# Entmax of the second batch: its power issued a step earlier in the mixture of experts

## The chip, the cores and the metric

The kernel runs on one NeuronCore of a Trainium2 chip. Five instruction streams work side by side: TensorE (PE in the profile, its weight loads as PEld), VectorE (DVE), ScalarE (ACT), GpSimd (POOL) and SyncE (SP), which issues most of the DMAs. They wait for each other through semaphores. The metric is the device time of one execution in microseconds; the time before is the median of three runs, 2685.04 us (2682.86 to 2685.15).

## The reference

The kernel is a two-layer decoder on `x` of 2 batches x 1024 tokens x 256, all in float32, each sublayer followed by a layer norm of the sum with its input: attention, cross attention with an MLP, a mixture of experts, attention again, cross attention again, and a feed-forward with fake quantisation. What matters here is the mixture of experts:

```python
logits = (xt @ Wr + br) / TEMP              # 2048 tokens x 8 experts
gates = entmax_bisect(logits)               # alpha = 1.5: p = max(x/2 - tau, 0)^2, sums to 1
gates = jnp.where(gates > THRESH, gates, 0.0)
h = jax.nn.relu(jnp.einsum('td,edf->etf', xt, W1) + b1[:, None, :])
y = jnp.einsum('etf,efd->etd', h, W2) + b2[:, None, :]
out = jnp.einsum('etd,te->td', y, gates)
```

Every expert is computed for every token and weighted by its gate. For alpha = 1.5 the threshold tau has a closed form over the sorted logits, with one square root per candidate; the kernel uses that in place of the bisection.

## The kernel before

The tokens are worked on in four groups `g` of 512; groups 0 and 1 are the first batch, 2 and 3 the second. The experts' stage (`l0_ffn`, line 806) runs 33 rounds `n` over `steps = (expert, group)`, expert outermost. Round n computes the hidden layer of step n and at the same time the second product of step n - 1. "First step" is n = 0, "second step" n = 1, "third step" n = 2, as one counts from one.

Both products use a Strassen-like scheme: seven products of half-sized blocks in place of eight, with sums of blocks as operands. The hidden layer's products are written (z, k) here: half z, block product k (matmuls at line 885, results in PSUM tiles `unit`). The second product's are written as plain k (matmuls at line 933, results in the PSUM tiles `acc` for k = 1, 6, 7, 4 and `bank` for k = 2, 5, 3). One tile takes its products one after the other, each added onto the last; VectorE reads it between two of them (line 942, scaled by the gate), and the next product on that tile can begin only when that read is over. The order of the 21 products in a round is a list, with positions i from 0:

```python
order = (
    (0, 1), (0, 2), (1, 1), (1, 2), 1, (0, 6), 2, (0, 5), (1, 6), 6, (1, 5), (0, 7), 5, (1, 7),
    7, (0, 3), (0, 4), 4, (1, 3), (1, 4), 3,
)
```

What each position issues beside its matmuls: ScalarE copies units to SBUF for k = 1, 6, 7 (lines 892, 896, 898) and applies the relu (874); VectorE adds units for k = 2, 7, 3 (lines 894, 899, 902), finishes k = 4 (908) and reads the second product (942). At the end of a round `sums` (line 914) forms the operand sums of the step just made: lines 783 and 784 on VectorE, then 785 and 786 on GpSimd. Line 783's result is needed by product 5 of the next round, 785's by product 6, 786's by product 3, 784's by product 7.

A dictionary `jobs` maps positions to other work, called right after the product at that position. The entmax is a generator, `self.entmax(b)` (line 712), cut into pieces by `yield`. For the second batch (`gates`, line 954) the pieces are called here: 1 and 2, four `max` each (line 743); 3, four small VectorE instructions (lines 746 to 749); 4, seven more (751 to 758) and then the square root, a power with exponent 0.5 of 128 x 64 elements on GpSimd (759); 5, four VectorE instructions of which the first reads the power's result (761 to 764); 6, seven more that finish the gates (766 to 772). The gates of the second batch are first read at the start of round n = 3 (`begin`, line 836).

TensorE, VectorE and ScalarE take their instructions in the order in which this code issues them (`manual_schedule`, line 967). GpSimd's and SyncE's queues are ordered by the framework's planner, by priority and by when it expects their inputs. An engine works through its queue in order: an instruction that waits holds all that is behind it.

Of the kernel before, what the change touches and what calls it, by code (L numbers as in the profile page):

```python
# [32 lines left out]
class Decoder:  # L33
# [772 lines left out]
    def l0_ffn(self):  # L806
        nc, t = self.nc, self.t
        HT = GT // 2
        with ExitStack() as s:
# [6 lines left out]
            def load(e):  # L816
                w1[e] = self.weight(t["L0_ffn_W1"][e].rearrange("(c p) f -> p c f", p=P), 2, 4 * D)
                w2[e] = self.weight(t["L0_ffn_W2"][e].rearrange("(f p) d -> p f d", p=P), 8, D)

            def first(e):  # L820
                w, h = w1.pop(e), 2 * D
                sums = self.gp.tile([P, 3, h], F32, tag="w1s", name="w1s")
                up[e] = self.left(
                    (nc.gpsimd, nc.gpsimd), w[:, 0, 0:h], w[:, 1, 0:h], w[:, 0, h : 2 * h],
                    w[:, 1, h : 2 * h], [sums[:, k, :] for k in range(3)],
                )

            def second(e):
                w, h = w2.pop(e), D // 2
                sums = self.gp.tile([P, 3, 4, h], F32, tag="w2s", name="w2s")  # L830
                down[e] = self.right(
                    nc.gpsimd, w[:, 0:4, 0:h], w[:, 0:4, h:D], w[:, 4:8, 0:h], w[:, 4:8, h:D],
                    [sums[:, k] for k in range(3)],
                )

            def begin(b):
                gT = one.tile([E, S], F32, tag="gT", name="gT")
                for h in range(2):
                    ps = self.bank()
                    for i in range(4):  # L840
                        nc.tensor.transpose(
                            ps[0:E, i * P : (i + 1) * P], self.gates[b][:, 4 * h + i, :], self.ident
                        )
                    self.evac(gT[:, h * GT : (h + 1) * GT], ps[0:E, :])
                    yield
                for h in range(2):
                    g = 2 * b + h
                    a = accs[g] = self.rp.tile([P, 4, D], F32, tag="r", name="r")
                    for i in range(0, 4, 2):
                        ps = self.bank().rearrange("p (i d) -> p i d", i=2)  # L850
                        for k in range(2):
                            n = h * 4 + i + k
                            nc.tensor.matmul(
                                ps[:, k, :], lhsT=gT[:, n * P : (n + 1) * P], rhs=self.mb2,
                                start=True, stop=True,
                            )
                        nc.vector.tensor_tensor(
                            a[:, i : i + 2, :], ps, self.x[g][:, i : i + 2, :], ALU.add
                        )
                    yield  # L860
# [53 lines left out]
            def sums(e, g):  # L914
                h = act.pop((e, g))
                s = one.tile([P, 3, 4, HT], F32, tag="hs", name="hs")
                engines = (nc.vector, nc.vector if (e, g) == steps[-1] else nc.gpsimd)
                return self.left(
                    engines, h[:, 0:4, 0:HT], h[:, 4:8, 0:HT], h[:, 0:4, HT:GT],
                    h[:, 4:8, HT:GT], [s[:, k] for k in range(3)],  # L920
                )

            def gather(e, g, h):

                ps = [None, None]

                def product(k):
                    at = int(k in (2, 5, 3))
                    if k in (1, 2):
                        ps[at] = self.bank() if at else self.acc()  # L930
                    for m in range(2):
                        for c in range(4):
                            nc.tensor.matmul(  # L933
                                ps[at][:, m * P : (m + 1) * P], lhsT=h[k][:, c, m * P : (m + 1) * P],
                                rhs=down[e][k][:, c, :], start=k in (1, 2, 5) and m + c == 0,
                                stop=True, skip_group_check=True,
                            )
                    i, d = {1: (0, 0), 2: (0, 0), 6: (0, 1), 3: (0, 1), 4: (1, 0), 5: (1, 1), 7: (1, 1)}[k]
                    for m in range(2):
                        a = accs[g][:, 2 * i + m, d * P : (d + 1) * P]  # L940
                        gate = self.gates[g // 2][:, g % 2 * 4 + 2 * i + m, e : e + 1]
                        nc.vector.scalar_tensor_tensor(  # L942
                            a, ps[at][:, m * P : (m + 1) * P], gate, a, ALU.mult, ALU.add
                        )

                return product
# [7 lines left out]
            gates = self.entmax(1)  # L954
# [5 lines left out]
            def normed(g):  # L960
                self.x[g] = self.layernorm(accs[g])

            def turned(g):
                nxT[g] = self.transposed(self.x[g])

            engines = {mybir.EngineType.PE, mybir.EngineType.DVE, mybir.EngineType.Activation}
            with self.tc.manual_schedule(engines=engines):
                start = [begin(b) for b in range(B)]
                mixed = None
                for n in range(len(steps) + 1):  # L970
                    jobs = {}
                    for k in range(4):
                        if n in (0, 3):
                            jobs[k] = lambda: next(start[n // 3])
                    if n == 0:
                        jobs[5], jobs[9] = self.last_group
                    if n in (1, 2):
                        for k in range(3):
                            jobs[4 + 4 * k] = lambda: next(gates)
                    if n > 3:  # L980
                        jobs[14] = lambda: next(ready, None)
                    if n >= len(steps) - NG + 2:
                        g = n - (len(steps) - NG + 2)
                        if n < len(steps):
                            jobs[5], jobs[17] = (lambda: normed(g)), (lambda: turned(g))
                    a = hidden(*steps[n]) if n < len(steps) else None
                    b = gather(*steps[n - 1], mixed) if n else None
                    if n % NG == 1 and n // NG + 1 < E:
                        load(n // NG + 1)
                    for i, k in enumerate(order):  # L990
                        if isinstance(k, int):
                            if b:
                                b(k)
                        elif a:
                            a(*k)
                        if i in jobs:
                            jobs[i]()
                    if n == 0:
                        for _ in start[0]:
                            pass  # L1000
                        self.tokens(2)
                        self.tokens(3)
                    if n == 2:
                        for _ in gates:
                            pass
                    if n % NG == NG - 1 and n // NG + 1 < E:
                        first(n // NG + 1)
                    if n % NG == 0 and 0 < n < len(steps):
                        second(n // NG)
                    if a:  # L1010
                        mixed = sums(*steps[n])
                for _ in ready:
                    pass
                for g in range(2, NG):
                    normed(g)
# [738 lines left out]
```

## Time and profile before

| | us |
|---|---|
| median of three runs | 2685.04 |
| the profiled execution's own time | 2682.37 |
| its span, first to last instruction | 2680.6 |
| TensorE busy | 2562.0 (96%) |
| VectorE busy | 1641.2 (61%) |
| ScalarE busy | 1151.9 (43%) |
| GpSimd busy | 798.1 (30%) |
| mean granted TensorE clock | 0.97 |
| one power of the entmax on GpSimd, line 759 | 10.55 |
| `sums` on VectorE, line 783, median of 32 | 1.218 |
| `sums` on GpSimd, line 786, median of 31 | 2.350 |

The profile is of one execution. Times in it count from the start of the span. A timeline row gives start, length, engine, line of the kernel, operation, output and inputs with their shapes, and how many instructions are merged; in brackets stands how long the engine had been idle before, and what ended that. The granted clock is the share of full speed that TensorE was given. TensorE's lengths are modelled from pipelined matmuls, so neighbouring rows overlap a little.

### The profile page before, as it was taken

The numbers are of one execution on the slowest core, as the hardware profiler recorded it, in microseconds if no ns is written. First come the engines' busy times: TensorE is split into PE (matmuls) and PEld (weight loads), VectorE is DVE, ScalarE is ACT, GpSimd is POOL, SyncE is SP. The second block draws the span as 40 slices with busy tenths as digits, with TensorE's granted clock in tenths as the row PEclk, the third lists the DMA queues.
The fourth block names the chain that finished last, engine by engine and source line by source line (L and its number), as shares of the span: only waits on it lengthen the run. The fifth ranks groups of instructions, "written<-read, shape, count | busy, mean of one in ns | idle before, by whom it ended". The sixth has DMA issues, their size and how long they took to land. (4 is left out here: it accounts for less than half of the span.)

```text
span 2680.6 us, 41386 instructions
## 1 busy us (share of the span) xinstructions
PE 2562.0 (96%) x16113; PEld 1910.0 (71%) x16113; DVE 1641.2 (61%) x3204; ACT 1151.9 (43%) x1808; POOL 798.1 (30%) x615
## 2 busy tenths in 40 slices
PE   8999999999999999899999999999979999998975
PEld 5777777777777656688999999999954444444652
DVE  4666566666656532245555565554667978895686
ACT  4555455545545522122333333333315655664344
POOL 3344344334444321242333333342311000100421
PEclk9999999999999999998999999999988999999996
DMA  4223223222322020100010010010030321110000
GB/s 123 60 56 83 54 54 70 60 54 64 76 54 50 15 75 16 34 5 17 24 32 17 27 33 32 12 44 5 1 61 3 59 37 32 32 33 1 1 1 32
DMA packets 87906, 102.95 MB, mean 38 GB/s; under 512 B 39496, under 2 KB 57504, under 8 KB 87712
## 3 DMA queue, kind: packets, MB, share of 16 engines
q1 hardware_dynamic: 87200, 99.27, 16.2%
q8 instruction: 128, 2.10, 0.3%
q10 hardware_dynamic: 512, 1.05, 0.2%
q14 instruction: 66, 0.54, 0.1%
HBM read 34.21 MB, written 2.10 MB: 14 GB/s over the span
## 5 line engine op out<-in xcount | busy, mean ns | idle before, releaser
L339 POOL TENSOR_SCALAR p<-p,rs 128x1024 f32<-128x1024 f32 x256 | 287.1, 1122 | 524.2 <-DVE rs L338 524.1
L1126 DVE TENSOR_REDUCE most<-bank 128x1 f32<-128x512 f32 x512 | 325.9, 685 | 55.2 <-PE bank L1120 47.1
L325 DVE TENSOR_REDUCE nm<-wide 128x1 f32<-128x1024 f32 x256 | 311.8, 1219 | 65.2 <-PE wide L311 44.6
L330 ACT ACTIVATE p<-wide,nm 128x1024 f32<-128x1024 f32 x256 | 286.1, 1118 | 96.3 <-DVE rs L338 85.2
L1169 ACT ACTIVATE w<-wide 128x1024 f32<-128x1024 f32 x256 | 248.3, 1022 | 138.1 <-PE wide L1163 129.4
L74 ACT COPY w<-bank 128x512 f32<-128x512 f32 x260 | 152.2, 586 | 321.6 <-PE bank L352 317.2
L352 PEld LDWEIGHTS bank<-ident,p 128*128 128x128 f32 x2048 | 232.6, 141 | 66.8 <-POOL p L339 25.0
L352 PE MATMUL bank<-ident,p 128*128 128x128 f32 x2048 | 270.8, 275 | 3.7 <-ACT w L74 2.2
L311 PE MATMUL wide<-k,q 128*128 128x512 f32 x960 | 252.4, 404 | 3.4 <-ACT p L330 3.4
L70 DVE COPY w<-bank 128x512 f32<-128x512 f32 x260 | 179.1, 689 | 107.7 <-PE bank L352 98.9
L373 PE MATMUL acc<-w,v 128*64 128x256 f32 x2048 | 237.8, 384 | 0.1
L874 ACT ACTIVATE mhT<-mhT,cols 128x256 f32<-128x256 f32 (+1 forms) x256 | 143.2, 607 | 149.9 <-DVE mhT L902 98.9
L373 PEld LDWEIGHTS acc<-w,v 128*64 128x64 f32 x2048 | 143.1, 137 | 76.5 <-issue 12.7
L311 PEld LDWEIGHTS wide<-k,q 128*128 128x128 f32 x960 | 171.2, 189 | 36.5 <-ACT p L330 5.4
L885 PE MATMUL unit<-xT,w 128*128 128x256 f32 x768 | 183.5, 381 | 0.0
L785 POOL TENSOR_TENSOR hs<-hs,mhT 128x1024 f32<-128x1024 f32 x31 | 103.4, 3336 | 262.0 <-DVE hs L783 262.0
L942 DVE SCALAR_TENSOR_TENSOR r<-acc,gates,r 128x128 f32<-128x128 f32 x256 | 77.8, 346 | 140.5 <-PE acc L933 140.5
L1120 PE MATMUL bank<-kst,qst 64*128 64x512 f32 x512 | 149.6, 483 | 12.4 <-DVE most L1126 12.1
L1120 PEld LDWEIGHTS bank<-kst,qst 64*128 64x128 f32 x512 | 70.3, 193 | 121.4 <-DVE most L1126 95.2
L885 PEld LDWEIGHTS unit<-xT,w 128*128 128x128 f32 x768 | 141.3, 191 | 17.2 <-issue 0.7
L181 POOL TENSOR_TENSOR rstd<-ve,nhalf 128x4 f32<-128x4 f32 (+2 forms) x28 | 26.1, 932 | 391.6 <-DVE ve L179 391.2
L1183 PE MATMUL acc<-w,v 128*32 128x512 f32 x1024 | 137.0, 607 | 0.0
(321 smaller groups left out, 4412.1 us busy)
## 6 DMA issues: line engine op xcount, KB each, us to landing
k<-xg SPq DMA_DIRECT2D x240, 128.0 KB, 2.4
w<-in_L_ffn_W SPq DMA_DIRECT2D x16, 1024.0 KB, 5.3
q<-xg SPq DMA_DIRECT2D x120, 128.0 KB, 2.3
qst<-qh SPq DMA_DIRECT2D x60, 64.0 KB, 2.4
qst<-ql SPq DMA_DIRECT2D x60, 64.0 KB, 2.4
kst<-kh SPq DMA_DIRECT2D x60, 64.0 KB, 2.9
kst<-kl SPq DMA_DIRECT2D x60, 64.0 KB, 2.4
xg<-in_x SPq DMA_DIRECT2D x4, 512.0 KB, 4.4
```

The costliest lines, as they stand in the source:

```text
L70: nc.vector.tensor_copy(out, in_)
L74: nc.scalar.copy(out, in_)
L311: nc.tensor.matmul(sc[h][:, kb, :], lhsT=qs[u, h, qt // 4][:, at : at + P], rhs=ks[u, h][i][:, kb * 512 : (kb + 1) * 512], start=i == 0, s ...
L325: nc.vector.tensor_reduce(nm, sc, AX.XY, ALU.max, negate=True)
L330: nc.scalar.activation(p, sc.rearrange("p a c -> p (a c)"), AF.Exp, bias=nm, accum_out=sum_)
L339: nc.gpsimd.tensor_scalar(p, p, rs, 1.0, ALU.mult, ALU.mult)
L352: nc.tensor.transpose(ps[:, k * P : (k + 1) * P], p[:, kt * P : (kt + 1) * P], self.ident)
L373: nc.tensor.matmul(av[rows, 0:256], lhsT=vals[u][:, kt, rows], rhs=turned[m, h][:, kt, :], start=kt == 0, stop=kt == 7,)
L885: nc.tensor.matmul(v[:, m, :], lhsT=up[e][k][:, f : f + P], rhs=self.halves[g][k], start=k in (1, 2, 5) and m == 0, stop=True, skip_group_ ...
L1120: nc.tensor.matmul(sc[a], lhsT=stack[b, jp, "q"][rows, q0 : q0 + P], rhs=stack[b, jp, "k"][rows, kb * 512 : (kb + 1) * 512], start=True, s ...
L1126: nc.vector.tensor_reduce(most[n][:, kb, qt, h : h + 1], sc[a], AX.X, ALU.max, negate=True)
L1169: nc.scalar.activation(slot[:, k, :], ps[k].rearrange("p a q -> p (a q)"), AF.Exp, scale=0.25)
```

## The change

Before, pieces 1, 2, 3 of the second batch's entmax were called at positions 4, 8, 12 of the second step (n = 1) and pieces 4, 5, 6 at positions 4, 8, 12 of the third (n = 2). After, pieces 1, 2, 3, 4 are called at positions 4, 7, 10, 13 of the second step, and pieces 5 and 6 at positions 8 and 12 of the third. The power belongs to piece 4, so it is issued in the second step, after (1, 7); the first reader of its result stays where it was, after (1, 6) of the third step. No instruction is added, removed or changed in size.

```diff
                     if n == 0:
                         jobs[5], jobs[9] = self.last_group
-                    if n in (1, 2):
-                        for k in range(3):
-                            jobs[4 + 4 * k] = lambda: next(gates)
+                    for k in {1: (4, 7, 10, 13), 2: (8, 12)}.get(n, ()):
+                        jobs[k] = lambda: next(gates)
                     if n > 3:
                         jobs[14] = lambda: next(ready, None)
```

## The prediction

> **What bounds the kernel now.** I read the page first, then the waits of the stretch around the change, then the timelines of TensorE, VectorE and GpSimd there, then the stretch in slices of 4 us. Part 1 of the page:
>
> ```profile
> PE 2562.0 (96%) x16113; PEld 1910.0 (71%) x16113; DVE 1641.2 (61%) x3204; ACT 1151.9 (43%) x1808; POOL 798.1 (30%) x615
> ```
>
> TensorE is busy for 96% of the span, so a gap in its row is lost time until shown otherwise. (The chain that ended last covers a few per cent at the kernel's end and says nothing here.) The waits between 1140 and 1230 us (total, times, longest):
>
> ```profile
> DVE esq L761 <- POOL esq L759: 10.1, 1, 10.1
> ...
> PE acc L933 <- DVE r L942: 5.9, 1, 5.9
> ```
>
> VectorE stands 10.1 us for the power, and TensorE 5.9 us for an L942 queued behind it. TensorE's timeline (start, length, engine, line; in brackets idle before and what ended it):
>
> ```profile
> 1165.33 1.95 PE L933 MATMUL acc<-w,mhT 128*128 128x128 f32 x16
> ...
> 1181.17 1.95 PE L933 MATMUL acc<-w2s,mhT 128*128 128x128 f32 x16
> ...
> 1184.68 1.95 PE L933 MATMUL bank<-w,hs 128*128 128x128 f32 x16
> ...
> 1189.92 1.95 PE L933 MATMUL acc<-w,mhT 128*128 128x128 f32 x16
> ...
> 1208.35 3.79 PE L933 MATMUL acc<-w,mhT 128*128 128x128 f32 x16 [5.95 <-DVE r L942]
> 1211.93 1.61 PE L885 MATMUL unit<-xT,w1s 128*128 128x256 f32 x4
> ...
> 1217.76 1.95 PE L933 MATMUL bank<-w,hs 128*128 128x128 f32 x16
> ```
>
> Product 1 starts at 1165.33 in the second step and 1189.92 in the third: an undisturbed step is 24.59 us. Product 3 of the third starts at 1217.76; 1184.68 + 24.59 = 1209.27 was its due time. So the stall costs **8.49 us**: 5.95 idle, 3.79 - 1.95 = 1.84 and 1.61 - 1.03 = 0.58 of slow matmuls after it, 0.12 of overlap. The slices (columns: length; PE, PEld, DVE, ACT, POOL busy; clock; DMA share, GB/s) show why they are slow: the granted clock is 0.50.
>
> ```profile
> 1205.00:1209.00 4.00, 0.65 (x3) 0.65 (x4) 2.11 (x8) 0.07 (x1) 1.75 (x1) 0.66 0.00 0
> 1209.00:1213.00 4.00, 4.00 (x18) 3.82 (x18) 3.08 (x12) 2.22 (x5) 0.00 (x0) 0.50 0.00 0
> ```
>
> VectorE's and GpSimd's timelines:
>
> ```profile
> 1178.47 0.69 DVE L899 TENSOR_TENSOR mhT<-unit,mhT 128x512 f32<-128x512 f32 x1
> 1179.64 0.61 DVE L942 SCALAR_TENSOR_TENSOR r<-acc,gates,r 128x128 f32<-128x128 f32 x2 [0.48 <-PE acc L933]
> ...
> 1187.19 1.22 DVE L783 TENSOR_TENSOR hs<-mhT 128x1024 f32<-128x1024 f32 x1
> ...
> 1192.43 2.04 DVE L751 TENSOR_TENSOR es<-es 128x128 f32<-128x128 f32 x1
> ...
> 1206.79 0.23 DVE L761 TENSOR_TENSOR esq<-emean,esq 128x64 f32<-128x64 f32 x1 [10.14 <-POOL esq L759]
> ...
> 1253.52 1.80 DVE L783 TENSOR_TENSOR hs<-mhT 128x1024 f32<-128x1024 f32 x1
> ```
> ```profile
> 1188.55 3.34 POOL L785 TENSOR_TENSOR hs<-hs,mhT 128x1024 f32<-128x1024 f32 x1 [18.01 <-DVE hs L783]
> 1191.97 2.35 POOL L786 TENSOR_TENSOR hs<-mhT,hs 128x1024 f32<-128x1024 f32 x1
> 1196.21 10.54 POOL L759 TENSOR_TENSOR esq<-u,eroot 128x64 f32<-128x64 f32 x1 [1.89 <-DVE u L758]
> ```
>
> The power takes 10.54 us. GpSimd is idle for 18.01 us before L785: the hole into which it moves.
>
> [...] L751 took 2.04 beside L786, 0.29 in the first batch's entmax; L783 took 1.80 at 1253.52 beside GpSimd's sums of weights, 1.22 elsewhere; L785's 3.34 is 2.22 behind L784 (1188.44 to 1189.67). L942 and L894, with one operand in PSUM, kept 0.61 and 1.28 beside L785 and L786. [...] the trace shows 0.50 after 5.95 us. [...]
>
> **The change part by part.** Positions i and pieces as in the text above; no DMA moves, and SP's queue is not touched.
> - Piece 2 to i=7, piece 3 to i=10. Between i=7 and 8 VectorE gets nothing: 0. Piece 3 (L746 to L749, 1177.52 to 1178.54) now follows L942 of product 6, which ends at 1174.09; VectorE is free there until 1175.82: 0.
> - Piece 4 to i=13 of the second step. Its seven instructions queue behind the L899 that ends at 1179.16 and take 1.86 (L751 to the next instruction: 1078.96 to 1080.83 in the first batch; GpSimd idle then too). Behind them stands L942 of product 7, which then starts at 1181.06 for 1179.64 and ends at 1181.67. Product 4 writes the same accumulator and waits for it: due 1181.17, now about 1181.72, **+0.55**. Everything after shifts by that. VectorE's delay itself dies in its gaps of 0.91, 0.26, 0.17 before 1187.
> - The power then runs from 1181.2 to 1191.7. Cover: L899, L902, L908, L942 have a PSUM operand. Not covered: L783 and L784 (two SBUF inputs) are due at 1187.75 and are held to 1191.6: **4 us late**, ending at 1192.8 and 1194.0. Next late are the two L894 (1194.6, 1195.2), L942 of product 1 (1195.8), and L785, behind both the power and L783: held by L784 to 1194.0, plus 2.22 is 1196.2. Who waits on TensorE: (0,5) needs the first L894, due 1194.35 + 0.55 = 1194.9, margin 0.3; product 6 needs L785 and that L942, due 1196.63, margins 0.4 and 0.8. So 0. If these margins go, each us late is a us of path.
> - Third step: piece 4 leaves i=4. Piece 5 (i=8) finds the power done 4 us ago, but L786 (1196.3 to 1198.5) holds its L761; done by 1199.5. L942 of product 6 then ends at 1200.1; product 7, which waits for it, is due at 1202.8: 0. Piece 6 stays at i=12: L942 to the L899 behind it was 2.18 (1208.81 to 1210.99), so L942 of product 7 ends at 1205.5; product 4 is due at 1206.3: 0.
>
> Not shown by the trace of before: the power beside a working VectorE (VectorE was idle through both). If L783 and L784 can go first, the power ends 2.44 later at 1194.1, L785 at about 1196.4: still in time. It can't be quicker than alone for the path, since nothing waits for its end before 1191.6. I take 0, with 0 to +3. Second, the slow clock that the fourth step's opening brings on: from the slices it lost 1.12 + 2.00 + 0.28 = 3.4 us of clock there (0.72, 0.50, 0.93) and 5.1 in the first step (0.93, 0.50, 0.50, 0.79); its phase may change, so -1.7 to +1.7, taken as 0.
>
> **Sum.** -8.49 + 0.55 = -7.94. Against the profiled execution, 2682.37 (span 2680.6 and 1.8 around it): 2674.4. The median of the runs is 2.67 above that execution: 2685.04 - 7.94 = **2677.1**, -0.30%. Nothing after this stage runs by the clock on the wall: later loads wait for TensorE's progress, so the gain keeps.
>
> **Rivals.**
> - *The power is covered in part.* The hold on L783 eats the margins of 0.3 and 0.4, and TensorE waits 2 to 4 us before (0,5) or product 6. For: 4 us is much, and the margins are small. Against: at 1253 to 1257 L783 and L784 were held 0.58 and 0.95 and the step was still 24.60 (1256.25 to 1280.85). With 3 us: 2680.1.
> - *The stall only moves a step forward:* L902 and L908 are locked out too, from 1181.2 to 1191.7. Then (0,1) of the third step has no free unit until about 1193.2, 6.2 us idle and 2.5 of slow clock: -7.9 + 8.7 is +0.8, 2685.8. Against it stand L942's 0.61 and L894's 1.28 beside GpSimd.
> - *Slower: the power takes much longer in company.* At 2.2 times, 23.2 us, it holds L783 until 1204.2, the first L894 ends at 1207.3, and (0,5) waits 12.4 us plus 2.5 of slow clock: -7.9 + 14.9 = +7.0, 2692.0. It decides from 1.5 times (16 us) on, where (0,5) comes at 1200.4 and the gain is used up. For: it was never seen in company. Against: L786 beside L942 kept 2.35.
> - *The change doesn't do what it says:* GpSimd's queue is ordered by the planner, and the power could stay behind L785 and L786. It would then start about 1194.4 for 1196.2: about -1.5, 2683.5. Against: L785 waits for L783, which VectorE reaches after L758, so the power is ready first.
>
> **How the numbers follow.** Chances: forecast 0.74, partly covered 0.12, stall moved 0.04, slower 0.06, order kept 0.04. The forecast's own range, from the clock's 1.7 and the runs' scatter of 2.3 us, is 2674 to 2680. For 8 in 10 the range takes in most of the partly covered case: 2673.5 to 2683. A measurement of this kernel tells 0.2% (5.4 us, from 2679.7 down) from no change. Faster: 0.70 of the forecast's 0.74 and 0.05 of the partly covered, 0.75; slower 0.06; the rest 0.19.
>
> **What would show it.** Right: the power at about 1181 ahead of L785, no wait of L761 for it; product 4 of the second step about 0.5 late; L783 of that step some 5 us long instead of 1.22, or the power some 13; L785 ending before 1196.6; no gap over 1 us on TensorE and a clock of 1.00 until product 3 of the third step near 1209.8. Wrong: a gap at (0,5) or product 6 of the third step, a power well over 13 us, L902 or L908 over 2 us, or a longer slow-clock stretch at the fourth step's opening.

## The result

| | before | after |
|---|---|---|
| median of 6 runs, us | 2683.95 | 2675.39 |
| lowest to highest | 2682.03 to 2687.35 | 2671.55 to 2675.82 |
| the profiled execution's own time | 2682.37 | 2675.75 |
| its span | 2680.6 | 2673.9 |

The ratio is 0.9964, with a 95% interval of [0.9952, 0.9977]: the kernel became 8.6 us faster. 2677.1 had been forecast, from a median of 2685.04.

The engines' busy times, part 1 of the page of after:

```profile
PE 2561.0 (96%) x16110; PEld 1907.9 (71%) x16113; DVE 1639.8 (61%) x3204; ACT 1152.8 (43%) x1808; POOL 798.7 (30%) x615
```

TensorE's busy sum hardly moved (2562.0 before), though the span is 6.7 us shorter: most of what went was idle time. In the waits between 1140 and 1230 us of after, TensorE's wait for L942 reads (total, times, longest):

```profile
PE acc L933 <- DVE r L942: 0.3, 1, 0.3
```

Those 5.9 us before are 0.3 us now, and they are another wait, as TensorE's timeline of after shows:

```profile
1165.64 1.95 PE L933 MATMUL acc<-w,mhT 128*128 128x128 f32 x16
...
1181.91 2.05 PE L933 MATMUL acc<-w2s,mhT 128*128 128x128 f32 x16 [0.26 <-DVE r L942]
...
1190.77 1.95 PE L933 MATMUL acc<-w,mhT 128*128 128x128 f32 x16
...
1196.93 1.95 PE L933 MATMUL acc<-w2s,hs 128*128 128x128 f32 x16
...
1203.09 1.95 PE L933 MATMUL acc<-w,mhT 128*128 128x128 f32 x16
...
1210.12 1.95 PE L933 MATMUL bank<-w,hs 128*128 128x128 f32 x16
```

Product 7 of the third step, which stood at 1208.35 behind 5.95 us of idle time and took 3.79, comes at 1203.09 without a gap and takes 1.95. The one gap left is 0.26 us before product 4 of the second step, which now waits for an L942 behind piece 4.

From product 1 of the second step to product 3 of the third it was 52.43 us before (1165.33 to 1217.76) and is 44.48 now (1165.64 to 1210.12): **7.95 us less**, where -8.49 + 0.55 = -7.94 had been worked out. Outside the stretch the two profiled executions differ by 1.3 us the other way (0.3 before it, 0.9 after it), which is within the scatter of the runs. The slices that had clocks of 0.66 and 0.50 are at full clock (columns as before: length, busy times, clock, DMA):

```profile
1204.00:1208.00 4.00, 4.00 (x31) 3.79 (x30) 3.31 (x9) 2.24 (x4) 0.00 (x0) 1.00 0.00 0
1208.00:1212.00 4.00, 4.00 (x30) 3.79 (x30) 2.17 (x5) 1.34 (x3) 0.00 (x0) 1.00 0.00 0
```

GpSimd's and VectorE's timelines of after:

```profile
1181.42 10.55 POOL L759 TENSOR_TENSOR esq<-u,eroot 128x64 f32<-128x64 f32 x1 [10.55 <-DVE u L758]
1191.92 2.36 POOL L785 TENSOR_TENSOR hs<-hs,mhT 128x1024 f32<-128x1024 f32 x1
1194.36 2.35 POOL L786 TENSOR_TENSOR hs<-mhT,hs 128x1024 f32<-128x1024 f32 x1
```
```profile
1188.04 1.22 DVE L783 TENSOR_TENSOR hs<-mhT 128x1024 f32<-128x1024 f32 x1
1189.29 1.23 DVE L784 TENSOR_TENSOR mhT<-mhT 128x1024 f32<-128x1024 f32 x1
...
1195.93 0.87 DVE L761 TENSOR_TENSOR esq<-emean,esq 128x64 f32<-128x64 f32 x1
```

The power starts at 1181.42, ahead of L785, and has ended 4 us before L761 asks for it. But L783 and L784 are not late: they took 1.22 and 1.23 in the middle of the power, where the prediction had them held to its end. L761 on the other hand took 0.87 in place of 0.23, beside L786.

### The profile page after: what moved, and what is told of

Read it like the earlier page. It is cut to its first block, busy times and chain, and to the rows that moved or that the text cites. A ratio compares the mean times of both kernels' runs of the same rounds, so it can differ in the third digit from the quotient of the medians.

```text
span 2673.9 us, 41384 instructions
## 1 busy us (share of the span) xinstructions
PE 2561.0 (96%) x16110; PEld 1907.9 (71%) x16113; DVE 1639.8 (61%) x3204; ACT 1152.8 (43%) x1808; POOL 798.7 (30%) x615
## 5 line engine op out<-in xcount | busy, mean ns | idle before, releaser
L785 POOL TENSOR_TENSOR hs<-hs,mhT 128x1024 f32<-128x1024 f32 x31 | 102.5, 3307 | 246.3 <-DVE hs L783 246.3
L942 DVE SCALAR_TENSOR_TENSOR r<-acc,gates,r 128x128 f32<-128x128 f32 x256 | 77.8, 345 | 140.6 <-PE acc L933 140.6
```

## The experiments

The measure in most of them is the stretch from product 1 of the second step to product 3 of the third on TensorE, free of what happens elsewhere in 2.7 ms. Undisturbed it is 43.95 us (the kernel without the power, below); the last column is the stretch less that. Whole times scatter by some us from run to run; they are compared with runs of the kernel before on the same chip (17 or 43 of them; for mid_issue and add_behind one). Diffs are against the changed kernel, the first one against the kernel before. Times since the span's start differ between kernels by some us for the same reason.

| kernel | the stretch, us | longest gap in it | lost to idle and clock |
|---|---|---|---|
| before | 52.43 | 5.95 | 8.48 |
| after | 44.48 | 0.26 | 0.53 |
| no_power | 43.95 | 0 | 0 |
| reader_later | 43.94 | 0 | 0 |
| early_issue | 43.95 | 0 | 0 |
| mid_issue | 45.06 | 0.85 | 1.11 |
| late_issue | 48.23 | 2.36 | 4.28 |
| short_wait | 48.90 | 3.03 | 4.95 |
| twice | 55.02 | 7.85 | 11.07 |
| add_behind | 44.48 | at product 4, as in after | 0.53 |

**The cause taken away.** The power of the second batch becomes a multiplication, where it stood before:

```diff
-        nc.gpsimd.tensor_tensor(sq, u, self.root, ALU.pow)
+        nc.gpsimd.tensor_tensor(sq, u, self.root, ALU.pow if b == 0 else ALU.mult)
```

> The kernel before with the second batch's power replaced by a multiplication of the same tile, pieces where they were (so the second batch's gates are not the reference's). It removes the wait's cause and nothing else. Theory: TensorE's gap in the third step and its slow clock vanish, product 3 of the third step comes 8.5 us earlier, ratio about 0.9969, as much as any placement can gain. If part of the changed kernel's gain came from elsewhere, it gains less than the changed kernel.

Measured: ratio 0.9968 [0.9953, 0.9984], 2675.91 against 2684.92. The stretch is 8.48 us shorter, as expected. GpSimd's timeline of this kernel:

```profile
1198.59 0.32 POOL L759 TENSOR_TENSOR esq<-u,eroot 128x64 f32<-128x64 f32 x1 [1.88 <-DVE u L758]
```

0.32 us for 10.54: the power was the whole of the stall, and the changed kernel has all of it but 0.53 us.

**Where the power runs, or who waits for it?** It stays in the third step; only its readers move back.

```diff
-                    for k in {1: (4, 7, 10, 13), 2: (8, 12)}.get(n, ()):
+                    for k in {1: (4, 8, 12), 2: (4, 17, 19)}.get(n, ()):
```

> The power stays in the third step (piece 4 at position 4, as before); only its readers move back, piece 5 to position 17 and piece 6 to 19. If the cost was VectorE standing behind the power's first reader (my theory), the whole stall goes although the power isn't issued earlier: the power runs from about 1196.2 to 1206.8, piece 5 comes at about 1208.4 and finds it done, no gap on TensorE in the third step, product 3 of the third step at about 1209.3 (8.5 us before the kernel before), time 8 us shorter, ratio about 0.997. If the gain came from starting the power in GpSimd's idle stretch of the second step, or from taking piece 4 out of the third step's VectorE queue, little or nothing is gained: ratio 0.999 to 1.000.

Measured: ratio 0.9959 [0.9944, 0.9974], 2673.73 against 2684.44. VectorE and GpSimd in its timeline:

```profile
1196.90 10.54 POOL L759 TENSOR_TENSOR esq<-u,eroot 128x64 f32<-128x64 f32 x1 [1.88 <-DVE u L758]
```
```profile
1208.46 0.61 DVE L942 SCALAR_TENSOR_TENSOR r<-acc,gates,r 128x128 f32<-128x128 f32 x2 [0.91 <-PE acc L933]
1208.98 0.21 DVE L761 TENSOR_TENSOR esq<-emean,esq 128x64 f32<-128x64 f32 x1
```

The power runs at the same place as before the change, and has been done for 1.5 us when L761 comes; the stall is gone entirely. So the gain comes from the distance between the power and its first reader on VectorE's queue. GpSimd's idle stretch in the second step is one way to get it, not the reason. It costs a little elsewhere: the gates come so late that the first transposes of the fourth step wait 0.27 us for them, and L853 0.73 for the copy behind.

**The 0.5 us that the change adds.** Pieces 2, 3 and 4 move further forward, into an idle stretch of VectorE.

```diff
-                    for k in {1: (4, 7, 10, 13), 2: (8, 12)}.get(n, ()):
+                    for k in {1: (4, 5, 6, 7), 2: (8, 12)}.get(n, ()):
```

> Pieces 1 to 4 at positions 4, 5, 6, 7 of the second step, 5 and 6 at 8 and 12 of the third as in the changed kernel. Piece 4 then falls into VectorE's idle stretch before product 6's L942 (about 1171.8 to 1173.7) instead of standing ahead of product 7's. If the delay of product 4 in the second step (0.74 us late in the changed kernel) is piece 4 queued ahead of L942, product 4 starts 15.84 us after product 1 of that step as in the kernel before, not 16.27, and the time is 0.4 to 0.7 us shorter than the changed kernel's: ratio to the kernel before about 0.9966. The power runs from about 1173.8 to 1184.3 and L785 of that step starts at once behind L783. If that delay has another cause it stays.

Measured: product 4 of the second step comes 15.84 us after product 1 (after: 16.27), and the stretch is the undisturbed one. VectorE in its timeline, where L758 ends piece 4:

```profile
1174.34 0.29 DVE L751 TENSOR_TENSOR es<-es 128x128 f32<-128x128 f32 x1
...
1176.09 0.20 DVE L758 TENSOR_SCALAR u<-u 128x64 f32<-128x64 f32 x1
1176.26 0.61 DVE L942 SCALAR_TENSOR_TENSOR r<-acc,gates,r 128x128 f32<-128x128 f32 x2
...
1182.42 0.61 DVE L942 SCALAR_TENSOR_TENSOR r<-acc,gates,r 128x128 f32<-128x128 f32 x2 [0.48 <-PE acc L933]
```

L942 of product 7 (the last row) waits for its product again, not for piece 4. The whole time, 2676.64 against 2684.44, ratio 0.9969 [0.9958, 0.998], can't tell this half microsecond from the changed kernel: the intervals overlap almost wholly. The trace shows it; the run times don't.

**The margin on the other side.** How late may the power be issued? Three and four positions later than in the changed kernel, and with the power doubled:

```diff
-                    for k in {1: (4, 7, 10, 13), 2: (8, 12)}.get(n, ()):
+                    for k in {1: (4, 7, 10, 17), 2: (8, 12)}.get(n, ()):    # late_issue
+                    for k in {1: (4, 7, 10, 16), 2: (8, 12)}.get(n, ()):    # mid_issue
```
```diff
         nc.gpsimd.tensor_tensor(sq, u, self.root, ALU.pow)
+        if b == 1:
+            nc.gpsimd.tensor_tensor(sq, u, self.root, ALU.pow)              # twice
```

> As the changed kernel, but piece 4 at position 17 of the second step. The power then runs from about 1185.8 to 1196.3. Theory of the margin: L785 of that step stands behind it, runs to about 1198.7, and product 6 of the third step, due at about 1196.1, waits for it: a gap of about 2.6 us on TensorE and no slow clock, gain over the kernel before about 5.9 us. If the power also holds L783 and L784 (due about 1187.2) as a GpSimd add does, both come at 1196.3 and the first L894 at about 1199.2: then (0,5), due at 1194.4, waits 4.9 us and the clock falls, gain about 1 us. VectorE's L783 beside the power tells: 1.22 us long without the hold, about 9 with it.

> Between the changed kernel and late_issue: piece 4 at position 16 of the second step. The power then runs from about 1184.1 to 1194.6, L785 to about 1197.0, and product 6 of the third step, due about 1196.1, waits about 0.9 us. late_issue's gap of 2.36 us brought the slow clock (1.9 us lost), the changed kernel's of 0.26 didn't. If 0.9 us is too short to bring it, product 1 of the second step to product 3 of the third is about 44.9 us (43.95 undisturbed); if any gap near 1 us does, about 46.8.

> The changed kernel with the second batch's power issued twice in a row on GpSimd (same inputs, same output). GpSimd is then taken from about 1181.4 to 1202.5, and L785 behind it ends at about 1204.9. Theory: the margin that the changed kernel lives on is L785 before product 6 of the third step, which is due at 1196.9; with 10.5 us more TensorE idles about 8.0 us there and 2.5 us of slow clock follow, time 10 us longer than the changed kernel, about 2 us longer than the kernel before. If the power holds VectorE's instructions with two SBUF inputs, L783 of the second step is 3 to 14 us long; if not, 1.22.

Measured: late_issue ratio 0.9984 [0.9977, 0.9991], twice 1.0002 [0.9993, 1.0012] (2686.11 against 2684.92); mid_issue was timed once, 2676.85 against 2687.57. TensorE in the timelines of late_issue, mid_issue and twice, in this order:

```profile
1198.53 3.06 PE L933 MATMUL acc<-w2s,hs 128*128 128x128 f32 x16 [2.36 <-POOL hs L785]
```
```profile
1198.31 2.05 PE L933 MATMUL acc<-w2s,hs 128*128 128x128 f32 x16 [0.85 <-POOL hs L785]
```
```profile
1204.78 3.78 PE L935 MATMUL acc<-w2s,hs 128*128 128x128 f32 x16 [7.85 <-POOL hs L787]
```

In all three it is product 6 of the third step that waits, for L785 (L787 in the numbering of twice) behind the power: the margin that the prediction named. In the changed kernel L785 ends at 1194.28 (1191.92 + 2.36) and product 6 comes at 1196.93, so 2.65 us were left, not 0.4. VectorE and GpSimd of late_issue show why:

```profile
1187.60 1.22 DVE L783 TENSOR_TENSOR hs<-mhT 128x1024 f32<-128x1024 f32 x1 [0.16 <-issue]
...
1196.20 2.35 DVE L761 TENSOR_TENSOR esq<-emean,esq 128x64 f32<-128x64 f32 x1 [1.12 <-POOL esq L759]
```
```profile
1185.62 10.55 POOL L759 TENSOR_TENSOR esq<-u,eroot 128x64 f32<-128x64 f32 x1 [15.16 <-DVE u L758]
1196.13 2.34 POOL L785 TENSOR_TENSOR hs<-hs,mhT 128x1024 f32<-128x1024 f32 x1
```

L783 is 1.22 beside the power again, and in mid_issue and twice as well; L761 beside L785 is 2.35. My expectation for late_issue missed in one thing: after the gap of 2.36 us the clock did fall. The stretch lost 4.28 us, 1.92 more than the gap, and product 6 took 3.06; in mid_issue, after a gap of 0.85, it took 2.05, and the clock was 1.00 in the slices from 1196 to 1204. A slice of late_issue shows the clock at 0.65:

```profile
1200.00:1204.00 4.00, 4.00 (x18) 3.60 (x18) 2.03 (x5) 0.00 (x1) 0.90 (x1) 0.65 0.02 4
```

In twice 11.07 - 0.53 - 7.85 = 2.7 us went to slower matmuls: product 6 took 3.78 for 1.95, and the four matmuls after it 1.77 for 1.03.

**A shorter wait of the old kind.** The power as before, pieces 5 and 6 a little later, so that fewer products stand behind the wait.

```diff
-                    for k in {1: (4, 7, 10, 13), 2: (8, 12)}.get(n, ()):
+                    for k in {1: (4, 8, 12), 2: (4, 12, 16)}.get(n, ()):
```

> As before but pieces 5 and 6 of the third step at positions 12 and 16. VectorE still waits for the power, which ends at about 1206.8, but with four fewer products queued behind it. The first product that needs the queue behind is product 4 (it waits for L942 of product 7): due about 1205.8, possible about 1209. So TensorE idles about 3 us in place of 5.95. If the slow clock after the gap has to do with the length of the gap, the clock stays at 1.00 and the gain is about 8.5 - 3.2 = 5.3 us; if any gap brings it, about 2.5 us less: 2.8 us.

Measured: ratio 0.9987 [0.998, 0.9994], 2680.35 against 2684.44. TensorE in its timeline, and the slice after:

```profile
1207.21 2.92 PE L933 MATMUL acc<-w2s,mhT 128*128 128x128 f32 x16 [3.03 <-DVE r L942]
```
```profile
1208.00:1212.00 4.00, 4.00 (x18) 3.63 (x17) 2.75 (x12) 1.13 (x2) 0.00 (x0) 0.57 0.00 0
```

VectorE waited 4.59 us and TensorE 3.03, at the product that had been named. The clock fell all the same, to 0.57: the gain in the stretch is 52.43 - 48.90 = 3.5 us, nearer to the 2.8 than to the 5.3.

**Does a GpSimd add hold L783 where the power doesn't?** The power is cut to half the tiles, and an add of 128 x 2048 follows. `long` is a weight tile set to zero in piece 1; the lines take the power's place for the second batch. The first form (long_add) put the add there with nothing to tie it:

```diff
+            nc.gpsimd.tensor_tensor(sq[:, 0:4], u[:, 0:4], self.root[:, 0:4], ALU.pow)
+            nc.gpsimd.tensor_tensor(sq[:, 4:8], u[:, 4:8], self.root[:, 4:8], ALU.mult)
+            nc.gpsimd.tensor_tensor(                                                # add_behind only
+                long[:, 0:64].rearrange("p (n e) -> p n e", e=E), sq, self.root, ALU.mult
+            )
+            nc.gpsimd.tensor_tensor(long, long, long, ALU.add)
```

> The changed kernel with the second batch's power split: the first 4 of its 8 tiles by the power (about 5.3 us), the other 4 by a multiplication (0.2 us), then one GpSimd add of 128 x 2048 (about 4.5 us) on a scratch tile; so the gates of half the tokens of the second batch are not the reference's. GpSimd is taken as long as in the changed kernel, but from about 1187 to 1191.5 with an add, beside which L783 falls due at 1188. If adds hold VectorE's instructions with two SBUF inputs and the power doesn't, L783 is about 4.5 us long here against 1.22 in the changed kernel, and nothing on TensorE changes, because the margins of the prediction (0.3 and 0.4 us) just hold: gap at (0,5) or product 6 of the third step 0 to 0.5 us. If neither holds, L783 is 1.22.

> As long_add, where the planner ran the add long before (at 1138.5, 3.60 us), since nothing tied it to the power. Here a small multiplication that reads the power's result writes into the scratch tile first, so the add of 128 x 2048 stands behind the power: half power 5.4 us from about 1181.2, two multiplications of 0.25, the add from about 1187.3 to 1190.9. The gates of half the tokens of the second batch are again not the reference's. L783 of the second step is due at about 1187.8. If a GpSimd add holds a VectorE instruction with two SBUF inputs and the power doesn't, L783 is about 4.2 us long, against 1.22 beside the power in the changed kernel; the first L894 then ends about 1193.9 and (0,5) of the third step, due about 1194.9, starts on time: product 1 of the second step to product 3 of the third stays 44.5 us. If neither holds: 1.22.

long_add failed as an experiment: the planner moved the untied add to 1138.53, into the first step, and L783 took 1.22 with nothing on GpSimd beside it. In add_behind it stands where it should. GpSimd and VectorE there (line 794 is what is 783 elsewhere, 795 is 784, 796 is 785):

```profile
1174.40 5.43 POOL L765 TENSOR_TENSOR esq<-u,eroot 128x32 f32<-128x32 f32 x1 [10.55 <-DVE u L761]
...
1180.52 3.60 POOL L770 TENSOR_TENSOR w<-w 128x2048 f32<-128x2048 f32 x1
1185.35 3.34 POOL L796 TENSOR_TENSOR hs<-hs,mhT 128x1024 f32<-128x1024 f32 x1 [1.22 <-DVE hs L794]
```
```profile
1181.03 4.18 DVE L794 TENSOR_TENSOR hs<-mhT 128x1024 f32<-128x1024 f32 x1
1185.24 1.22 DVE L795 TENSOR_TENSOR mhT<-mhT 128x1024 f32<-128x1024 f32 x1
1186.38 1.28 DVE L905 TENSOR_TENSOR mhT<-unit,mhT 128x512 f32<-128x512 f32 x2
```

L783's sum is 4.18 us long beside the add (4.2 expected), against 1.22 beside the power at the same place in the queue. And a hold of 3 us costs TensorE nothing: the stretch is 44.48, that of the changed kernel. So the prediction's chain of margins stood as far as a hold of 3 us can test it (4 had been worked out), and only its cause was absent. The whole times of the two kernels, one run each (long_add 2673.45, add_behind 2668.86 against 2687.57), say nothing of the hold: add_behind was already 7.0 us ahead of the changed kernel where the stretch begins (1158.63 for 1165.64).

**A faster kernel.** early_issue, and the same cure for the first batch's power in the sublayer before, where VectorE's order is the planner's. Between 960 and 1960 us that wait was TensorE's longest in the kernel before (waits of that stretch):

```profile
PE bank L617 <- DVE r L621: 8.5, 1, 8.5
```

```diff
                     if g == 2:
                         steps = self.entmax(0)
-                    some()
+                    some(4)        # pieces 1 to 4; the calls after it, not shown, wait for the round of g = 3
...
-        nc.vector.tensor_tensor(sq, m, sq, ALU.subtract)
+        if b == 0:
+            minus = tile_("eminus", [P, 1])
+            nc.vector.tensor_scalar(minus, self.x[2][:, 0, 0:1], 0.0, -1.0, ALU.mult, ALU.add)
+            nc.vector.scalar_tensor_tensor(sq, sq, minus, m, ALU.mult, ALU.add)
+        else:
+            nc.vector.tensor_tensor(sq, m, sq, ALU.subtract)
...
+        if b == 0:
+            u = tile_("eu0", full)
         nc.vector.tensor_tensor(u, xs, srt[:, :, 0:1].to_broadcast(full), ALU.subtract)
```

> early_issue, and the same cure for the first batch in the sublayer before: there the power (1081 to 1091.5) also had VectorE standing, TensorE idle for 8.52 us before an L617 and slow for about 3 us after it. The first reader of the power is made to depend on the next group's layer norm by a factor of -1 computed from it, and piece 6 gets a tile of its own, so that the planner puts both behind that layer norm. If the wait is again the cause, that gap goes and the time is about 11 us below early_issue: ratio to the kernel before about 0.9925. If another wait takes its place (for the copies or the softmax of the next group), less.

Measured: 2662.1 (2660.41 to 2664.15) against 2684.92, ratio **0.9911 [0.9894, 0.9927]**, faster than both kernels. TensorE's timelines there, of after (whose first batch is as before) and of this kernel:

```profile
1080.95 3.62 PE L617 MATMUL bank<-w,xhT 128*128 128x256 f32 x16
1084.50 1.98 PE L593 MATMUL bank<-xpT,xv 64*128 64x512 f32 x4
1095.00 10.02 PE L617 MATMUL bank<-w,xhT 128*128 128x256 f32 x32 [8.52 <-DVE r L621]
1104.86 7.03 PE L604 MATMUL wide<-xoT,w 128*128 128x512 f32 x16
```
```profile
1084.85 3.62 PE L617 MATMUL bank<-w,xhT 128*128 128x256 f32 x16
1088.40 1.98 PE L593 MATMUL bank<-xpT,xv 64*128 64x512 f32 x4
1090.31 7.17 PE L617 MATMUL bank<-w,xhT 128*128 128x256 f32 x32
1097.33 7.03 PE L604 MATMUL wide<-xoT,w 128*128 128x512 f32 x16
```

From the first row to the last it is 23.91 us and 12.48 us: 11.4 less, as expected, and no other wait took its place. The other batch gives its 8.48 in the stretch of the table (43.95). Together that is 19.9 of the 22.8 us between the medians; between the profiled spans (2680.6 and 2661.5) it is 19.1. The difference of 3 us lies within the scatter of the runs.

## Why the prediction was right, and where not

- *The stall was worth 8.49 us.* Right: 8.48 with the power taken away, and 8.49 with its readers moved back.
- *Its split into 5.95 of idle and 2.5 of slow clock.* Right for this gap. But "each us late is a us of path" was too low, and the rival "covered in part" counted a gap of 3 us without any loss of clock: short_wait shows 1.92 more for 3.03, and late_issue 1.92 more for 2.36.
- *Piece 4 ahead of L942 costs 0.55.* The next step's product 1 came 0.54 late (25.13 - 24.59). Right, and early_issue shows that it is that queueing. Product 4 itself started only 0.43 late (16.27 - 15.84); the other 0.1 was lost just after it, where its matmuls took 2.05 for 1.95.
- *The power holds L783 and L784 for 4 us.* **Wrong.** This step was the author's estimate: it carried over to the power what the trace of before shows beside GpSimd's adds (L751 took 2.04 for 0.29, L783 1.80 for 1.22). L783 was 1.22 beside the power in the changed kernel, in mid_issue, in late_issue and in twice, and the power was 10.55 beside VectorE as alone. So the power did not hold these sums. Beside GpSimd's adds VectorE was late in the cases shown: L761 took 0.87 and 2.35 for 0.23, and L783's sum 4.18 for 1.22 in add_behind. The prediction had named an L783 of some 5 us, or a power of some 13, as a sign of being right; neither came. What the chain built on the hold was right as far as it could be tried: a hold of 3 us (add_behind) cost TensorE nothing. So the error cost the forecast nothing; it only made the margin of product 6 look like 0.4 us where it was 2.65, and gave the rival "covered in part" more weight than it had.
- *Then L785 and product 6 are next.* Right: in three kernels, product 6 behind L785 is what waits.
- *L761 held by L786 until 1198.5.* It was held, to 1196.8, since L785 and L786 came some 2 us earlier than worked out; it mattered to nobody in either form.
- *The fourth step's slow clock, taken as 0 with 1.7 to either side.* From product 3 of the third step to product 6 of the fourth the profiled executions show 20.06 us or 18.43, 1.63 apart: 20.06 before and 20.05 after, so 0 was right for this pair; no_power, both and long_add had 18.43 or 18.42, and reader_later 21.01, with its own waits in it.
- *Rivals.* That the stall only moves a step forward needed L902 and L908 to be locked out; beside the power they took 0.69 and 0.88 at most, as in the kernel before. That the power grows in company: 10.55, unchanged. That the planner leaves it behind L785: it came ahead.
- *Sum.* -7.94 worked out, -7.95 in the stretch, -8.6 between the medians, -6.6 between the profiled executions. The last two differ within the scatter of the runs. That the stretch agrees to 0.01 us is in part luck: product 4's own delay was 0.43 where 0.55 had been worked out, and the slower matmuls behind it made up for that.

## What to carry to other kernels

VectorE works through its queue in order: here it stood 10.14 us for the power, and an L942 queued behind that wait left TensorE idle for 5.95. So ask of each slow result how far its first reader stands behind it in the queue, and move either end; where the power ran mattered here only through what it delayed on its own engine (the stretch is 43.94 us with it in the third step, in reader_later, and 43.95 with it in the second, in early_issue). When it is moved, look for two new neighbours: what now stands behind the moved inputs (here half a microsecond of L942), and what is queued behind the moved work itself (here L785, with 2.65 us to spare). The waits of the kernel before hold a second stall of the same kind, worth more than the first: 11.4 us for 8.48.

## What the runs showed of the hardware

- GpSimd's power doesn't share the fate of its adds: a VectorE sum of 128 x 1024 with both operands in SBUF took 1.22 us beside the power and 4.18 beside an add that ran on for 3.1 us after it was issued. Why VectorE's sum stays at 1.22 us beside a power that reads two SBUF tiles was not tried: the power also reads far more slowly than the add, 64 elements per partition in 10.55 us where the add reads 2048 in 3.60, so the operation and the rate of reading are not told apart. It is shown in four kernels (after, late_issue, mid_issue, twice), with the sums L783 and L784 only (1.22 and 1.23 us).
- A gap of less than 3 us was followed by the slow clock too: 0.65 after 2.36 us of idle time in late_issue (1.92 us lost), 0.57 after 3.03 in short_wait (1.92 lost), 0.50 after 5.95 in the kernel before; after 0.85 in mid_issue and 0.26 in after the clock was 1.00. Between 0.85 and 2.36 the runs say nothing, and the longer gaps were each seen in one profile. The clock also fell without a long gap: at the fourth step's opening in after, where the matmuls of line 853 contract over 8 rows, no gap was longer than 0.21 us, and the clock was 0.53 and 0.61. What brings it there was not tried.

```profile
1215.74 1.99 PE L853 MATMUL bank<-mb,gT 8*128 8x256 f32 x8 [0.21 <-DVE gT L70]
```
```profile
1220.00:1224.00 4.00, 4.00 (x18) 3.32 (x17) 1.27 (x2) 0.00 (x0) 0.00 (x0) 0.53 0.02 4
1224.00:1228.00 4.00, 4.00 (x21) 3.64 (x21) 0.61 (x2) 0.59 (x1) 0.00 (x0) 0.61 0.00 0
```

- The power costs 10.55 us for 64 elements per partition, 5.43 for 32 and 1.01 for 4 (the layer norm's, line 181, with exponent -0.5); a multiplication of the same 64 costs 0.32.
